# A relational graph layer on one core: inner Winograd products from the second matrix on, edge counts in half a PSUM bank, and relation counts from the slot table

## The chip, the cores and the metric

One core of one Trainium2 chip. The metric is the device time of one execution of the program in microseconds (us), as a median over runs. A profile is one execution of the same program with the hardware profiler on; its times are shown in microseconds from the span's start. In its rows PE is TensorE's matmuls, PEld its weight loads, DVE is VectorE, ACT is ScalarE, POOL is GpSimd, and SP is SyncE, which here only issues DMAs.

## The reference

There are N = 1250 nodes with D = 1024 features, and E = 20000 edges with a source, a destination (sorted) and one of R = 8 relations. Everything is fp32.

```python
h = relu(layernorm(x))
out = h @ root + bias
for r in range(8):                       # mean over the edges of relation r into each node
    mask = (edge_type == r)
    sums = segment_sum(h[src] * mask[:, None], dst, N)
    cnt  = segment_sum(mask, dst, N)
    out += (sums / max(cnt, 1)[:, None]) @ weight[r]
u = out
z = concat([u, h], axis=1) @ w_gate + b_gate
y = x + tanh(u) * z + h * (1 - z)
```

## The kernel before

**Products first, edges after.** The kernel multiplies all nodes by each matrix and gathers rows of the products afterwards: `h @ weight[r]` goes to DRAM (`y0` for relations 0 to 4, `y1` for 5 to 7), and each edge later fetches one row of it, scaled by one over its count. There are eleven matrices: eight relations (matrix zero to seven), `root`, and two halves of `w_gate`. Nodes are ten blocks of 128 rows (`ND`), taken as five pairs i = 0 to 4, block i with block i + 5.

**Winograd's scheme, twice.** `product` multiplies two blocks of rows (256 x 1024) by one matrix (1024 x 1024) with seven quarter products instead of eight: `p1` to `p7`, each of a left factor (A11, A12, A22, S1 to S4, in `h_op`) and a right factor (in `wbuf`), with K = 512 and 512 columns, so four fp32 matmuls of 128x512 each. `Factors` makes the right sums T1 to T4 on VectorE. For two neighbouring i, and from matrix one on, some of the seven quarter products are joined over both i and split once more into 2x2 with seven inner products of two 128x256 matmuls each: class `Second` does A12 B21 so, in all matrices from one on; classes `Third` (S4 B22) and `First` (A11 B11) only where `thirds(s)` holds, which is `s > EARLY`, with EARLY = 3. These classes take their sums from VectorE, and ScalarE copies inner results between PSUM and SBUF in the middle of the chain: `First.early` and `First.late` are two halves of one inner product, the early one at the end of the `product` before; `Third.first` writes into the PSUM bank `ps_q`, and `Third.hold` uses `ps_n`. The other PSUM banks are four of `ps` and two of `ps_b` (`lead`).

**Work beside the products.** The order is written out by hand. `product` calls `done()` after each quarter product (and after some fills, the pieces of inner products put between them), which calls `between(j)`; that takes one step of a generator. So there are seven steps in each `product`, and whatever a generator emits up to its `yield` lies behind that piece of TensorE's work on every engine's own queue. From matrix zero to three the generator is `index()`: `columns` and the layer norms, then `slots`, then `order`.

**The edge index (`slots`).** Edges stand in 157 chunks of 128; four chunks make a group (`CG`), so there are 40 groups, and a group takes two steps. The index gives each edge its place among the edges of its key (node and group of relations, 20 blocks of keys). In a group, `one_hots` makes bf16 one-hot matrices (ScalarE for `is_lo`, VectorE for `is_at`), `count` multiplies them (four matmuls of 128x100: 20 columns for keys and 80 for relation and block), `seen` holds running counts by VectorE additions, `as_int`, `split` and `as_bf16` cut the counts into two bf16 parts, and `place` looks up each edge's count with four matmuls of 128x40, adds the rank within the chunk, and scatters edges into `table` in DRAM by indirect DMA, 28 slots for each key (`SLOTS`), and behind them the eight relation counts' reciprocals. The functions work on different groups in the same round:

```python
for j in range(ng + 3):
    for f, of in ((as_bf16, j - 3), (one_hots, j), (load_keys, j - 1), (as_int, j - 2),
                  (None, None), (count, j - 1), (split, j - 2), (place, j - 3),
                  (to_los, j - 2), (None, None)):
```

`(None, None)` is a `yield`. Counts are written into `ps_n`, look-ups into `ps_q`, one buffer each.

**After the index.** `order` ranks the nodes by count (`places`); `rows_and_weights` scatters the ranking and gathers each node's slots from `table` into `idx`; `weights` turns a slot's relation and the reciprocal counts into a factor for each slot. In matrix four the generator `beside_group` does this for both groups of relations; `passes_needed` decides, once, how many extra passes over the table are needed for nodes with many edges, and one branch (`tc.If`, L1443) does them if any. From matrix five on the edge phase runs: 193 gathers of rows of `y` by GpSimd's indirect DMA (L1294), each added by VectorE with its weight (L1299).

Of the kernel before, what the change touches and what calls it, by code (L numbers as in the profile page):

```python
# [9 lines left out]
F32 = mybir.dt.float32  # L10
# [9 lines left out]
def tile_rgcn_highway(  # L20
# [52 lines left out]
    WIDE = SLOTS + R  # L73
# [3 lines left out]
    NTB = R * ND  # L77
    FAR = 1 << 20
    CG = 4
    GOT = 5  # L80
# [34 lines left out]
    table = dram.tile([G * KEYS * WIDE, 1], I32, name="table")  # L115
# [142 lines left out]
    class Third:  # L258
# [31 lines left out]
        def first(self, p):  # L290
            self.b = psum.tile([P, CG, P], F32, name="ps_q", bufs=1).rearrange(
                "p c k -> p (c k)")[:, :H]
# [242 lines left out]
    def thirds(s):  # L535

        return s > EARLY

    waiting, waiting_third, waiting_first = {}, {}, {}
# [10 lines left out]
    def step(s, i, between=lambda j: None, second=None):  # L550
# [61 lines left out]
        def sums(j):  # L612


            e = waiting[0][0]
            for k in {2: (0, 1), 4: (2, 3)}.get(j, ()) if s > EARLY else (j,) if j < 4 else ():
                e.right(k)
            if j == (5 if s > EARLY else 4):
                e.left()
# [82 lines left out]
    idx = const.tile([P, G, ND, WIDE], I32, name="idx")  # L702
    rcp = idx.bitcast(F32)[:, :, :, SLOTS:]
# [4 lines left out]
    n_pass = const.tile([1, 1], I32, name="n_pass")  # L708
    apart = const.tile([P, 1], F32, name="apart")
# [20 lines left out]
    def slot_weights(g, at, w, t, drc):  # L730

        n = at.shape[2]
        for r in range(R0[g], R0[g + 1]):
            by, to = rcp[:, g, :, r], w
            if r > R0[g]:
                by, to = drc, t
                nc.vector.tensor_sub(drc, rcp[:, g, :, r], rcp[:, g, :, r - 1])
# [3 lines left out]
            if r > R0[g]:  # L741
                nc.vector.tensor_add(w, w, t)
        nc.vector.scalar_tensor_tensor(w, at, float(FAR), w, op0=OP.is_lt, op1=OP.mult)

    table_rows = table.rearrange("(k s) o -> k (s o)", s=WIDE)
    more_rows = table_more.rearrange("(k s) o -> k (s o)", s=MORE)

    def rows_and_weights(g):
# [16 lines left out]
        for d in range(ND):  # L765
            rows_of(idx[:, g, d, :], table_rows, node_key[:, g, d:d + 1])
            if d % 2:
                yield

    with ExitStack() as early:  # L770
# [103 lines left out]
        far = ix0.tile([P, G * ND * WIDE // 4], I32, name="far")  # L874
# [44 lines left out]
        tb_col = ix1.tile([P, NCH], F32, name="tb_col")  # L919
# [7 lines left out]
        pid = ix1.tile([P, 1], F32, name="pid")  # L927
        less_pid = ix1.tile([P, 1], F32, name="less_pid")
        before = ix1.tile([P, P], F32, name="before")
        runs = ix1.tile([P, NHI + NTB], F32, name="runs")  # L930

        def columns():
# [23 lines left out]
            blk_i = ix0.tile([P, 2, P], I32, name="blk_i")  # L956
            nc.vector.tensor_single_scalar(blk_i, ed["dst"], 7, op=OP.arith_shift_right)
            blk = ix0.tile([P, 2, P], F32, name="blk")
            nc.vector.tensor_copy(blk, blk_i)
# [3 lines left out]
            for g in range(1, G):  # L963
# [5 lines left out]
            tb = ix0.tile([P, 2, P], F32, name="tb")  # L969
            nc.vector.scalar_tensor_tensor(tb, f["typ"], float(ND), blk,  # L970
                                           op0=OP.mult, op1=OP.add)
# [3 lines left out]
            for of, to in ((key, key_col), (row, row_col), (tb, tb_col)):  # L975
# [12 lines left out]
            nc.vector.tensor_single_scalar(first, key_col, float(WIDE), op=OP.mult)  # L988
# [8 lines left out]
        def slots(ix):  # L997
# [3 lines left out]
            seen = {-1: ix.tile([P, CG, NHI + NTB], F32, name="seen", bufs=3)}  # L1001
            nc.vector.memset(seen[-1][:, CG - 1, :], 0.0)
            ng = -(-NCH // CG)

# [3 lines left out]
            def one_hots(j):  # L1008
# [8 lines left out]
                is_at = ix.tile([P, CG, NHI + NTB], BF16, name="is_at", bufs=4)  # L1017
                for t, of, width in ((is_at[:, :, :NHI], hi_col, NHI),
                                     (is_at[:, :, NHI:], tb_col, NTB)):
                    nc.vector.tensor_tensor(t[:, :m, :],  # L1020
                                            of[:, c0:c1, None].to_broadcast([P, m, width]),
# [691 lines left out]
```

## Time and profile before

| | |
|---|---|
| Time, median of 3 runs | 1348.01 us (1346.19 to 1349.48) |
| The profiled execution's own time | 1347.63 us |
| Its span, first to last instruction | 1345.6 us |
| Matmuls of 128x512 into `ps_b` (L405) | x1560 rows, 701.9 us busy |
| Matmuls of 128x256 of inner products (L218) | 71.5 us busy in the largest of several groups |
| Counting matmuls (L1031) / look-ups (L1082) | x157 each, 13.6 / 10.1 us busy |
| VectorE additions to `seen` (L1036) | x157, 40.3 us busy, 257 ns each |
| ScalarE one-hots (L1013) | x157, 50.2 us busy |

How to read it: an fp32 matmul instruction shows as two rows, so x8 of 128x512 are the four of one quarter product. A row's own duration is the time through the array; matmuls overlap, so the price of one is the distance from its start to the next one's start. "Idle before" with a name behind an arrow says which instruction on which engine ended the wait. A timeline row merges equal instructions that follow each other: start, length, engine, line, operation, output<-inputs, shapes, count.

### The profile page before, as it was taken

What the parts mean: (1) busy time and instruction counts of PE and PEld (TensorE: products, weight loads), DVE (VectorE), ACT (ScalarE), POOL (GpSimd) and SP (SyncE); (2) the same over time, 40 slices, a digit from 0 to 9 for tenths busy, and PEclk for the clock granted to TensorE, in tenths of its full rate; (3) what the DMA queues carried; (4) which work ended last, traced back from release to release, by engine and by line L of the source; (5) the groups of instructions that cost most, each with busy time, mean ns of one, the idle gap of its engine ahead of it and who ended that gap; (6) DMA issues with size and microseconds to landing.
All of it is one profiled execution on the core that took longest, in us unless ns stands there. A gap on an engine that the chain in (4) does not pass through costs nothing.

```text
span 1345.6 us, 13662 instructions
## 1 busy us (share of the span) xinstructions
PE 1332.0 (99%) x4098; PEld 712.2 (53%) x4098; DVE 995.7 (74%) x2049; ACT 384.0 (29%) x852; POOL 579.9 (43%) x511
## 2 busy tenths in 40 slices
PE   9999999999999999999999999999999999999997
PEld 5444455455445545655654565565556556554443
DVE  7855976876784937524887978887788799867875
ACT  3335656565641111111221211112122111221210
POOL 0001755655563346101444646336354655625631
PEclk9999999999999999999999999999999999999999
DMA  8744665844673162133739778867878967879961
GB/s 313 271 181 145 105 135 148 209 81 124 160 183 83 49 171 53 48 126 122 234 114 349 223 254 326 310 230 268 286 260 291 343 211 234 288 275 283 345 171 59
DMA packets 106910, 271.17 MB, mean 202 GB/s; under 512 B 22692, under 2 KB 24946, under 8 KB 106704
## 3 DMA queue, kind: packets, MB, share of 16 engines
q1 hardware_dynamic: 46640, 120.01, 29.2%
q0 software_dynamic: 44064, 118.28, 27.9%
q10 hardware_dynamic: 16128, 31.98, 7.2%
q8 instruction: 32, 0.52, 0.2%
q14 instruction: 46, 0.38, 0.1%
HBM read 212.71 MB, written 75.66 MB: 214 GB/s over the span
## 4 chain that ended last, share of the span: by engine, by line
PE 79%; issue 7%; DMA 7%; DVE 4%; POOL 3%; ACT 0%; POOLq 0%; DVEq 0%; ACTq 0%
PE ps_b L405 40%; PE ps L405 17%; PE ps L218 11%; DMA got<-y,idx 5%; PE ps_n L405 3%; PE ps_b L218 2%; PE ps_q L218 2%; PE ps_q L405 1%; DVE u L1299 1%; PE ps_n L218 1%; POOL got L1294 1%; DMA got<-hr_dram,node 1%; PE ps L370 1%; DMA hr_dram<-row 1%; POOL out_dram L720 1%
## 5 line engine op out<-in xcount | busy, mean ns | idle before, releaser
L405 PE MATMUL ps_b<-w,h_op 128*128 128x512 f32 x1560 | 701.9, 595 | 1.0 <-ACT row L484 0.8
L405 PEld LDWEIGHTS ps_b<-w,h_op 128*128 128x128 f32 x1560 | 291.6, 190 | 329.2 <-issue 318.7
L1294 POOL DMA_INDIRECT got<-y,idx x193 | 246.3, 1276 | 326.4 <-DVE u L1299 195.8
L1299 DVE SCALAR_TENSOR_TENSOR u<-got,w_of,u 128x1024 f32<-128x1024 f32 (+1 forms) x193 | 247.1, 1283 | 33.8 <-DMA got<-y,idx 31.1
L405 PE MATMUL ps<-w,h_op 128*128 128x512 f32 (+1 forms) x592 | 263.4, 588 | 1.0 <-ACT row L464 1.0
L1110 POOL DMA_INDIRECT table<-row_col,at_i x157 | 177.7, 1132 | 156.4 <-DVE at_i L1106 70.3
L405 PEld LDWEIGHTS ps<-w,h_op 128*128 128x128 f32 x592 | 111.3, 190 | 125.0 <-issue 120.8
L430 DVE TENSOR_TENSOR row<-row 128x512 f32<-128x512 f32 x53 | 36.7, 693 | 72.9 <-ACT row L429 72.7
L429 ACT COPY row<-ps_b 128x512 f32<-128x512 f32 x53 | 31.0, 585 | 197.4 <-PE ps_b L405 193.4
L514 ACT COPY row<-ps_b 128x512 f32<-128x512 f32 x49 | 28.6, 584 | 200.3 <-PE ps_b L405 171.5
L405 PE MATMUL ps_n<-w,h_op 128*128 128x512 f32 x176 | 80.1, 592 | 0.0
L218 PE MATMUL ps<-w,w 128*128 128x256 f32 x288 | 71.5, 381 | 0.3 <-DVE w L211 0.3
L484 ACT COPY row<-ps_b 128x512 f32<-128x512 f32 x54 | 31.6, 586 | 135.9 <-PE ps_b L405 131.1
L218 PE MATMUL ps<-w,h_op 128*128 128x256 f32 x264 | 68.3, 381 | 0.0
L218 PEld LDWEIGHTS ps<-w,w 128*128 128x128 f32 x288 | 54.2, 190 | 21.9 <-issue 14.6
L1036 DVE TENSOR_TENSOR seen<-seen,ps_n 128x100 f32<-128x100 f32 x157 | 40.3, 257 | 30.1 <-PE ps_n L1031 10.1
L218 PEld LDWEIGHTS ps<-w,h_op 128*128 128x128 f32 x264 | 49.6, 190 | 24.3 <-issue 18.7
L1096 DVE SCALAR_TENSOR_TENSOR junk<-k_bc,key_col,before 128x128 f32<-128x128 int32 x157 | 55.1, 351 | 4.2
L453 ACT COPY row<-ps_b 128x512 f32<-128x512 f32 x54 | 31.7, 587 | 90.9 <-PE ps_b L405 82.9
L405 PEld LDWEIGHTS ps_n<-w,h_op 128*128 128x128 f32 x176 | 33.4, 190 | 39.5 <-issue 38.7
L464 ACT COPY row<-ps 128x512 f32<-128x512 f32 x37 | 21.6, 585 | 105.2 <-PE ps L405 92.6
L173 DVE TENSOR_TENSOR w<-w,w 128x2048 f32<-128x2048 f32 (+1 forms) x12 | 25.4, 2115 | 35.1 <-PE ps L405 34.9
(244 smaller groups left out, 1530.6 us busy)
## 6 DMA issues: line engine op xcount, KB each, us to landing
y<-row SPq DMA_DIRECT2D x72, 512.0 KB
w<-in_L_gnn_weight_dram ACTq DMA_DIRECT2D x21, 1024.0 KB
w<-in_L_gnn_weight_dram SPq DMA_DIRECT2D x10, 1024.0 KB
k_bc<-keys_dram SPq DMA_DIRECT2D x39, 256.0 KB
l_bc<-los_dram SPq DMA_DIRECT2D x39, 256.0 KB
w<-in_L_gnn_w_gate_dram ACTq DMA_DIRECT2D x6, 1024.0 KB
h_dram<-h_op SPq DMA_DIRECT2D x9, 512.0 KB
u<-in_L_gnn_bias_dram SPq DMA_DIRECT2D x9, 512.0 KB
```

The costliest lines, as they stand in the source:

```text
L218: nc.tensor.matmul(p, a[:, k, :], b[:, k, :], start=(fresh and k == 0), stop=(k == 1), skip_group_check=True)
L405: nc.tensor.matmul(b[:, at], aop[:, i, k, :], w.of[i][:, k, at], start=(fresh and k == 0), stop=(k == KQ - 1), skip_group_check=True)
L429: nc.scalar.copy(d, b)
L430: nc.vector.tensor_add(c22, c22, d)
L453: nc.scalar.copy(c11, b)
L484: nc.scalar.copy(c12, b)
L514: nc.scalar.copy(c21, b)
L1036: nc.vector.tensor_add(seen[j][:, i, :], was, p[:, i, :])
L1096: nc.vector.scalar_tensor_tensor(junk, o["k_bc"][:, i, :], key_col[:, c:c + 1], before, op0=OP.is_equal, op1=OP.mult, accum_out=rank[:, c: ...
L1110: ins = nc.gpsimd.indirect_dma_start(out=table[:, :], out_offset=bass.IndirectOffsetOnAxis(ap=at_i[:n, i:i + 1], axis=0), in_=row_col[:n, ...
L1294: nc.gpsimd.indirect_dma_start(out=t[:n], out_offset=None, in_=y[g][:, :], in_offset=bass.IndirectOffsetOnAxis(ap=at[:n, d, k:k + 1], axis=0),
L1299: nc.vector.scalar_tensor_tensor(u[:n], t[:n], w, u[:n], op0=OP.mult, op1=OP.add)
```

## The change

It does four things.

- **Inner products from matrix one on.** `thirds(s)` is `s > 0` for `s > EARLY`; so A11 B11 and S4 B22 of the first two pairs of i get inner products in matrices one to three too. Their SBUF room is taken from the start on, and the T sums and left sums of `Second` lie at other steps there.
- **Counts by key alone.** The 80 columns for relation and block go, with all that made them (`tb`), so a count is 128x20. `seen` is a ring of twelve chunks. The two parts of a count are made without integers: a bf16 copy (ScalarE) and the residue (VectorE).
- **Half a bank, on zeros.** Counts and look-ups both lie in the right half of the bank `ps_q`, in matmuls that add to what is there; `clear`, a ScalarE copy of a zero, wipes 240 columns in each round. The left half is that of `Third.first`. `ps_n` is free for `Third.hold`.
- **Relation counts from the slot table.** In matrix four `slot_counts` counts, for each key, how many slots are at or above each relation's first row; reciprocals and slot weights follow in the last pair of matrix four. Nodes with more edges than slots are counted by a second branch (`counts_over`) ahead of it. The scatter to the table goes in bursts of four groups (`AT`).

The diff, cut to its core:

```diff
-            self.b = psum.tile([P, CG, P], F32, name="ps_q", bufs=1).rearrange(
-                "p c k -> p (c k)")[:, :H]
+            self.b = (q_bank[0] if q_bank else psum.tile([P, CG, P], F32, name="ps_q", bufs=1)
+                      .rearrange("p c k -> p (c k)"))[:, :H]
...
     def thirds(s):
-        return s > EARLY
+        return s > 0
...
-            for k in {2: (0, 1), 4: (2, 3)}.get(j, ()) if s > EARLY else (j,) if j < 4 else ():
+            for k in {2: (0, 1), 4: (2, 3)}.get(j, ()):
                 e.right(k)
-            if j == (5 if s > EARLY else 4):
+            if j == 5:
                 e.left()
...
+    def slot_counts(g, at, t, cum, to):
+        n = R0[g + 1] - R0[g]
+        nc.vector.memset(cum[:, :, 0:1], float(at.shape[2]))
+        for r in range(1, n + 1):
+            nc.vector.tensor_single_scalar(t, at, float(r * N), op=OP.is_ge)
+            nc.vector.reduce_sum(cum[:, :, r:r + 1], t, axis=AX.X)
+            yield
+        nc.vector.tensor_sub(to[:, :, R0[g]:R0[g + 1]], cum[:, :, :n], cum[:, :, 1:n + 1])
...
+            RING = 3 * CG
+            seen = ix.tile([P, RING, NHI], F32, name="seen", bufs=1)
+            counted = q_bank[0][:, H:H + CG * NHI].rearrange("p (c b) -> p c b", b=NHI)
+            looked = q_bank[0][:, H + CG * NHI:H + 3 * CG * NHI].rearrange(
+                "p (c a b) -> p c a b", a=2, b=NHI)
+
+            def clear():
+                nc.scalar.copy(q_bank[0][:, H:H + 3 * CG * NHI],
+                               zero.to_broadcast([P, 3 * CG * NHI]))
...
             def count(j):
                 cs, o = chunks(j), now[j]
-                p = psum.tile([P, CG, P], F32, name="ps_n", bufs=1)[:, :, :NHI + NTB]
-                for i in range(m):
-                    nc.tensor.matmul(p[:, i, :], o["is_lo"][:, i, :], o["is_at"][:, i, :],
-                                     start=True, stop=True)
...
+                for i in range(len(cs)):
+                    nc.tensor.matmul(counted[:, i, :], o["is_lo"][:, i, :], o["is_at"][:, i, :],
+                                     start=False, stop=True, skip_group_check=True)
+                for i, c in enumerate(cs):
+                    nc.vector.tensor_add(seen[:, c % RING, :], seen[:, (c - 1) % RING, :],
+                                         counted[:, i, :])
...
             def place(j):
-                p = psum.tile([P, CG, P], F32, name="ps_q", bufs=1).rearrange("p c k -> p (c k)")
                 for i in range(m):
-                    nc.tensor.matmul(p[:, i * 2 * NHI:(i + 1) * 2 * NHI], o["to_lo"][:, i, :],
+                    nc.tensor.matmul(looked[:, i].rearrange("p a b -> p (a b)"),
+                                     o["to_lo"][:, i, :],
                                      o["s_b"][:, i].rearrange("p a b -> p (a b)"),
-                                     start=True, stop=True)
+                                     start=False, stop=True, skip_group_check=True)
...
             for j in range(ng + 3):
-                for f, of in ((as_bf16, j - 3), (one_hots, j), (load_keys, j - 1), (as_int, j - 2),
-                              (None, None), (count, j - 1), (split, j - 2), (place, j - 3),
+                for f, of in ((one_hots, j), (load_keys, j - 1), (as_bf16, j - 2),
+                              (None, None), (count, j - 1), (residue, j - 2), (place, j - 3),
                               (to_los, j - 2), (None, None)):
                     if f is None:
                         yield
                     elif 0 <= of < ng:
                         f(of)
+                    if f is as_bf16:
+                        clear()
...
         def beside_group():
+            for _ in range(4):
+                yield
+            passes_over()
+            yield
+            yield from rows_and_weights(1)
+            yield
+            yield
             for g in range(G):
-                if g:
-                    yield from rows_and_weights(g)
-                    yield
-                    yield
-                weights(g)
+                yield from counts(g)
+
+        def weights_of_groups():
+            as_reciprocals()
+            yield
+            for g in range(G):
+                yield from weights(g)
                 yield
             yield from passes_needed()
...
         while s < R0[1]:
             step(s, i, on)
             s, i = next(steps)
+            if (s, i) == (R0[1] - 1, NP - 1):
+                for _ in ready:
+                    pass
+                counts_over()
+                ready = weights_of_groups()
```

## The prediction

> **What bounds the kernel now.** I read the page first, then TensorE's waits, then the granted clock and busy time by stretch, then the timeline of the stage in which the changed code runs.
>
> ```profile
> PE 1332.0 (99%) x4098; PEld 712.2 (53%) x4098; DVE 995.7 (74%) x2049; ACT 384.0 (29%) x852; POOL 579.9 (43%) x511
> PE   9999999999999999999999999999999999999997
> PEclk9999999999999999999999999999999999999999
> ```
>
> TensorE has something in flight in 99% of the span, in every slice but the last, at full granted clock. So every microsecond of matmul taken out can be won, and every wait put in front of TensorE is lost whole. Its waits in the whole run:
>
> ```profile
> PE ps L697 <- POOL eps L699: 1.4, 1, 1.4
> PE ps_q L1082 <- ACT s_b L1066: 1.4, 1, 1.4
> ```
>
> The list is seven lines long and 5.8 us in all; only one wait belongs to the edge index, one look-up at L1082. The index runs from 107 to 420 us beside the products. Matrix one and matrix four, by stretch (length, then busy time of PE, PEld, DVE, ACT, POOL):
>
> ```profile
> 140.50:264.00 123.50, 123.50 (x431) 61.72 (x430) 96.98 (x412) 75.81 (x201) 74.47 (x70) 1.00 0.68 149
> 506.00:622.00 116.00, 116.00 (x354) 66.50 (x353) 57.47 (x127) 21.40 (x43) 24.88 (x23) 1.00 0.25 83
> ```
>
> Matrix four already has the inner products that the change gives to matrices one to three, and takes 7.5 us less; but there VectorE is at 50% and ScalarE at 18%. In matrix one, with the index beside it, they are at 79% and 61%. How the index lies between the products now (start, length):
>
> ```profile
> 146.99 0.34 PE L1031 MATMUL ps_n<-is_at,is_lo 128*128 128x100 bf16 x4
> 147.17 0.26 PE L1082 MATMUL ps_q<-s_b,to_lo 128*128 128x40 bf16 x4
> 147.27 3.68 PE L405 MATMUL ps_b<-w,h_op 128*128 128x512 f32 x8
> 148.14 1.13 DVE L1036 TENSOR_TENSOR seen<-seen,ps_n 128x100 f32<-128x100 f32 x4
> ...
> 150.79 1.03 PE L218 MATMUL ps<-w,h_op 128*128 128x256 f32 x4
> 150.99 0.58 ACT L484 COPY row<-ps_b 128x512 f32<-128x512 f32 x1 [1.94 <-PE ps_b L405]
> ...
> 151.65 0.34 PE L1031 MATMUL ps_n<-is_at,is_lo 128*128 128x100 bf16 x4
> 151.69 0.70 ACT L1013 ACTIVATE is_lo<-io,less_lo 128x128 bf16<-128x128 f32 x2
> ```
>
> Four counts, four look-ups 0.18 us later, and the next product 0.10 us after that: 0.28 us a group, although VectorE reads the counts only at 148.14. The look-ups need nothing of these counts (they are for the group two before) and write another bank. This freedom is what the change gives up.
>
> **The change, part by part.**
>
> *Inner products.* A11 B11 and S4 B22 of two pairs in each of matrices one, two and three: 12 products, each 14 matmuls of 256 columns for 8 of 512. Four 512-wide instructions (x8 in the rows) follow each other in 3.43 us, 0.858 each; two 256-wide (x4) in 0.86, 0.430 each. 8 x 0.858 - 14 x 0.430 = 0.85 us; twelve give **-10.2 us**.
>
> *Narrower counts.* 157 matmuls of 20 columns for 100. Four counts take 0.18 us, four look-ups of 40 columns 0.10; at the look-ups' price 157 x (0.045 - 0.025) = 3.1 us, and the two transposes of `tb` (0.4 us at 46.8) go: **-3.5 us**. TensorE's work falls by 13.7.
>
> *The shared bank.* Counts and look-ups go into the right half of the bank `ps_q`, and the inner S4 B22 product into its left half. In the instruction order of the changed program the first look-up of each group still stands directly behind the group's four counts, but it now waits for VectorE, namely for the last of the four `seen` additions that read those very counts; this is so in all 38 groups that have both. Behind it on TensorE is the next product, and everything else. The price from the row where VectorE had nothing else to do:
>
> ```profile
> 196.90 0.34 PE L1031 MATMUL ps_n<-is_at,is_lo 128*128 128x100 bf16 x4
> 197.08 0.26 PE L1082 MATMUL ps_q<-s_b,to_lo 128*128 128x40 bf16 x4
> 197.28 1.13 DVE L1036 TENSOR_TENSOR seen<-seen,ps_n 128x100 f32<-128x100 f32 x4 [1.94 <-PE ps_n L1031]
> ```
>
> The additions start 0.38 us after the first count. With 20 columns for 100 each is shorter by 80 x 1.04 ns (a 512-wide addition takes 0.685, a 256-wide 0.42), so four end after 0.80 us for 1.13: at 198.08, and the look-up starts 0.05 later (the gap seen where TensorE waited for an engine: the copy's end at 1077.73, weight load at 1077.79). 198.13 for 197.08 is 1.05 us; 38 groups give **+40 us**. None of it has cover: TensorE's queue is in order.
>
> The Trainium skill's page "PSUM — Partial Sum Buffer", section "PSUM bank collisions raise a hardware error", says to guard PSUM by bank (and quadrant of partitions) and not by address, since two engines in one bank collide even in different columns. No run here shows a collision. Were only addresses to count, the sum would be the 13.7 us gained; by the page's rule the waits above are needed.
>
> *VectorE behind.* The 1.05 us holds when VectorE is idle; the first row above shows 148.14 - 146.99 = 1.15 us to the start, and another group had 175.76 - 173.39 = 2.37. For each of 39 intervals between groups I added the VectorE instructions queued in the changed order (durations from the groups by form) and set them against TensorE's work in the interval. Example, the sixth group: residue 0.24, own and sum 0.64, four ranks 1.74, four index steps 0.66, two T sums 1.37, one-hot 0.23, two row additions 0.85, the four sums for the next inner product 2.21: 7.94 against TensorE's 4.49, 3.45 late. Twelve intervals are late, **22 us** in all. The index itself got cheaper on VectorE (a group from 5.1 to 3.75 us: narrower one-hots and additions, one residue for two splits, index steps per four groups), some 54 us over 39 groups; the sums and additions of the inner products put 12 us on each of the pairs, 71 in all, most of it in the index's stretch.
>
> *ScalarE behind.* Before, the step ahead of a group's look-ups began with the cast that they need (L1066); now it runs four one-hots 1.28, their Relu 0.63, the copy of `seen` 0.24 and the new zeroing of the half bank (128x240; 128x256 costs 0.36): 2.5 us, and the next counts wait for that zeroing. Where a whole product lies between, 3.43 us cover it. Where only a fill of 0.86 us lies between, as in the rows at 150.79, they don't: copy 0.59 + 2.5 + hand-over 0.27 - 0.86 = 2.5 us. Nine groups stand so: some 24 us. Four times the inner product's first matmul into `ps_q` meets the same zeroing (some 14), and six early and late inner parts wait for a ScalarE copy that stands behind the burst (some 6). Together **44 us**; VectorE catches up meanwhile. With the larger of the two in each interval the sum is 54; the bounds are 22 (ScalarE wholly hidden) and 66 (no overlap). I take 50, near the interval count, since a TensorE that waits gives both queues some air.
>
> *Nothing on the path:* counts from the slot table (8 comparisons and sums, some 1 us each on VectorE, in matrix four with 58 us free), weights moved to the end of matrix four (three VectorE instructions per step of TensorE; their first use is in matrix five), the fourfold scatter bursts on GpSimd (16 x 1.29 us in some 30; the last has 13 scatters, 17 us, and the gather that needs them comes after four steps and ten `places` of 1.55 us, some 29 us), the missing DMA of relation counts to the table. The second branch: the first now costs TensorE a load and 0.23 us at 972.9 while its matmuls go on at 0.86 us steps, so 0; if its cover is gone, 1 us.
>
> *Sum:* the profiled execution took 1347.6 us (span 1345.6 and 2.0 around it), 0.4 below the median of 1348.0. 1347.6 - 13.7 + 40 + 50 = **1424 us**.
>
> **Rivals.**
> 1. *Only the floor counts.* While TensorE waits, VectorE and ScalarE work off their queues, and the late intervals shrink to about 8: 1347.6 - 13.7 + 40 + 8 = 1382. For it: neither engine is over 80% in the stretch, and a longer period gives both more. Against: the bursts are emitted right ahead of the group and after the product that releases them, so a pause elsewhere doesn't move them.
> 2. *Faster: the wait is met before it is reached.* If the readout is over within 14 us / 38 = 0.36 us of the last count, the matmuls decide and the time is 1334. Against: four dependent additions with 0.25 us before the first; the shortest seen is 1.38 us with 100 columns.
> 3. *Both queues feed each other.* ScalarE's zeroing waits for VectorE's reading of the look-ups, VectorE's for TensorE, TensorE's inner products for sums that stand behind ranks. With no overlap (66) and 15 us of such second-order waits: 1455.
> That the change isn't what it says: its matmul counts (96 fewer of 512, 168 more of 256) say that it is.
>
> **How the numbers follow.** Forecast 0.70; rival 1 0.16; rival 3 0.09; rival 2 0.04; 0.01 that gain and waits cancel. What a measurement here can tell from no change is about 0.2%, 2.7 us. The range runs from rival 1 (1380) to rival 3's value (1455). Faster 0.04, same 0.01, slower 0.95.
>
> **What would show it.** TensorE's waits should name VectorE's `seen` some 38 times at 1.05 us and more, and ScalarE's zeroing of `ps_q` ten times or so at 2 to 3 us; TensorE's slices should read 7 or 8 from 110 to 480 us and 9 after; matrix one should take 150 us or more, matrix four as now. Wrong would be: look-ups that follow the counts in under 0.3 us (rival 2), waits of 1.0 to 1.3 us throughout (rival 1), or a loss after 500 us, in which case the moved weights or the second branch cost what I put at nothing.

## The result, and the profile after

| | median | range | ratio to before |
|---|---|---|---|
| before | 1347.9 us | 1346.2 to 1349.5 | |
| changed, as recorded | 1520.8 us | 1514.1 to 1523.5 | 1.1276, 95% interval 1.1237 to 1.1315 |
| changed, unaltered, on chip 6 ("the second chip" below) | 1471.3 us | 1468.6 to 1475.2 | 1.0944, 1.0925 to 1.0964 |
| changed, unaltered, on chip 4 | 1513.3 us | 1510.6 to 1524.0 | 1.126, 1.1224 to 1.1295 |

The change makes the kernel slower, as forecast, but by 173 us and not by 76; the recorded time lies far above the range. The two reruns say that some 50 us of the 173 are not the program's alone: chip 6 ran without them, chip 4 with them, which is taken up below. Which chip the recorded run had is not on record. Without these 50 us the time is still above the range.

The page of the recorded run (busy time and share of each engine; the span in 40 slices of 38 us):

```profile
PE 1372.7 (90%) x4240; PEld 760.0 (50%) x4240; DVE 1018.5 (67%) x2012; ACT 395.8 (26%) x859; POOL 572.1 (38%) x510
PE   9998677668775779899999999999999999999997
PEclk9999888789988799999999999999999999999999
```

TensorE's row drops to between 5 and 8 from the fourth slice to the fifteenth. The granted clock drops with it, which the prediction didn't have. By stretch (length, then busy time of PE, PEld, DVE, ACT, POOL; granted clock, DMA share, GB/s): the stretch that begins with the counts at 146.99 and ends with those at 264.61 before (117.6 us), and matrix four (116.0 us before):

```profile
156.78:359.51 202.73, 140.89 (x461) 78.72 (x460) 94.38 (x359) 75.43 (x189) 64.55 (x64) 0.83 0.37 86
679.00:795.00 116.00, 116.00 (x355) 66.51 (x354) 58.71 (x120) 21.44 (x43) 27.55 (x26) 1.00 0.24 83
```

The first takes 203 us for 118, and TensorE works 141 of them. Matrix four takes what it took. TensorE's waits (us in total, times, longest):

```profile
PE ps_q L1095 <- DVE seen L1050: 74.8, 36, 10.0
PE ps_q L1047 <- ACT ps_q L1022: 15.5, 8, 3.8
PE ps_b L217 <- ACT ps_b L343: 6.2, 2, 4.9
PE ps_q L217 <- ACT ps_q L1022: 6.1, 2, 3.1
```

L1095 is the look-ups, L1050 the additions of counts, L1047 the counts, L1022 the zeroing, L217 the inner products. The first line is the wait that the prediction put first, 36 times. One group, to be read against the groups shown before:

```profile
186.12 0.26 PE L1047 MATMUL ps_q<-is_at,is_lo 128*128 128x20 bf16 x4 [2.91 <-ACT ps_q L1022]
186.49 0.17 DVE L1050 TENSOR_TENSOR seen<-seen,ps_q 128x20 f32<-128x20 f32 x1 [6.18 <-PE ps_q L1047]
186.88 0.59 DVE L1050 TENSOR_TENSOR seen<-seen,ps_q 128x20 f32<-128x20 f32 x3 [0.21 <-DVE seen L1050]
...
187.52 0.29 PE L1095 MATMUL ps_q<-s_b,to_lo 128*128 128x40 bf16 x4 [1.14 <-DVE seen L1050]
```

The counts wait 2.9 us for ScalarE's zeroing, the look-ups 1.1 us for VectorE's four additions. Before, the same eight matmuls took 0.28 us.

**An account of TensorE's time.** For each matmul I took the distance to the next one's start, and what it has above the undisturbed distance of its shape (0.429 us for 512 columns, 0.2155 for 256). Where a product matmul takes up to twice its distance, the excess is counted as half speed, otherwise as a stall.

| us | stalls | half speed | profiled execution |
|---|---|---|---|
| before | 10.3 | 7.8 | 1347.6 |
| changed, second chip | 120.1 | 32.5 | 1468.6 |
| changed, recorded | 159.0 | 45.6 | 1520.6 |

The column of half speed also catches small excesses that have nothing to do with the clock: the kernel before has 7.8 us there at a granted clock of 1.00 (7 to 1341 us), and none of its product matmuls takes about twice its distance. So only what lies above 7.8 is the clock's.

With the 13.7 us of work taken out, the second chip should be 109.8 + 24.7 - 13.7 = 120.8 us above before, and is 121.0; the recorded run should be 38.9 + 13.1 = 52.0 above that, and is 52.0. On the second chip the largest waits are these:

```profile
PE ps_q L1095 <- DVE seen L1050: 56.3, 38, 4.2
PE ps_q L1047 <- ACT ps_q L1022: 17.6, 9, 2.9
PE ps_q L217 <- ACT ps_q L1022: 9.6, 4, 3.0
```

So three things are to be explained: the stalls, the half speed, and what differs between chips.

### The profile page after: what moved, and what is told of

It is laid out like the page before. It is cut to its first block, busy times and chain, and to the rows that moved or that the text cites. A ratio compares the mean times of both kernels' runs of the same rounds, so it can differ in the third digit from the quotient of the medians.

```text
span 1518.8 us, 13834 instructions
## 1 busy us (share of the span) xinstructions
PE 1372.7 (90%) x4240; PEld 760.0 (50%) x4240; DVE 1018.5 (67%) x2012; ACT 395.8 (26%) x859; POOL 572.1 (38%) x510
## 4 chain that ended last, share of the span: by engine, by line
PE 67%; DVE 10%; issue 9%; another core or an unknown queue 5%; DMA 4%; ACT 3%; POOL 2%; POOLq 0%; DVEq 0%; ACTq 0%; SPq 0%
PE ps_b L404 32%; PE ps L404 11%; PE ps L217 11%; PE ps_n L404 4%; PE ps_b L217 3%; PE ps_q L217 3%; DVE seen L1050 2%; DMA got<-y,idx 1%; PE ps_q L404 1%; PE ps_n L217 1%; DVE junk L1172 1%; ACT is_lo L1033 1%; POOL got L1308 1%; PE ps L369 1%
## 5 line engine op out<-in xcount | busy, mean ns | idle before, releaser
L404 PE MATMUL ps_b<-w,h_op 128*128 128x512 f32 x1464 | 680.5, 611 | 1.0 <-ACT row L483 0.8
L1126 POOL DMA_INDIRECT table<-row_col,at_i x157 | 163.4, 1041 | 352.9 <-DVE at_i L1122 289.3
L404 PE MATMUL ps<-w,h_op 128*128 128x512 f32 (+1 forms) x448 | 202.2, 595 | 1.7 <-ACT row L463 1.7
L404 PEld LDWEIGHTS ps<-w,h_op 128*128 128x128 f32 x448 | 85.8, 193 | 97.1 <-issue 92.1
L404 PE MATMUL ps_n<-w,h_op 128*128 128x512 f32 x224 | 102.3, 593 | 0.0
L428 ACT COPY row<-ps_b 128x512 f32<-128x512 f32 x53 | 31.1, 586 | 243.4 <-PE ps_b L404 220.1
L1050 DVE TENSOR_TENSOR seen<-seen,ps_q 128x20 f32<-128x20 f32 x157 | 27.3, 174 | 93.3 <-PE ps_q L1047 47.2
L513 ACT COPY row<-ps_b 128x512 f32<-128x512 f32 x49 | 28.7, 586 | 227.6 <-PE ps_b L404 170.2
L1095 PE MATMUL ps_q<-s_b,to_lo 128*128 128x40 bf16 x157 | 10.6, 186 | 81.6 <-DVE seen L1050 74.8
L217 PE MATMUL ps<-inner,inner 128*128 128x256 f32 x288 | 78.1, 396 | 2.0 <-DVE inner L278 2.0
L217 PE MATMUL ps<-w,h_op 128*128 128x256 f32 x288 | 79.3, 400 | 0.0
L217 PE MATMUL ps<-w,w 128*128 128x256 f32 x288 | 73.1, 387 | 0.2 <-DVE w L210 0.2
L483 ACT COPY row<-ps_b 128x512 f32<-128x512 f32 x54 | 31.7, 586 | 157.8 <-PE ps_b L404 150.8
L217 PEld LDWEIGHTS ps<-w,h_op 128*128 128x128 f32 x288 | 56.5, 199 | 25.4 <-issue 18.7
L217 PEld LDWEIGHTS ps<-inner,inner 128*128 128x128 f32 x288 | 57.5, 200 | 18.7 <-issue 7.7
L217 PEld LDWEIGHTS ps<-w,w 128*128 128x128 f32 x288 | 55.4, 194 | 22.1 <-issue 14.3
```

Of the source, the lines that this page charges most:

```text
L217: nc.tensor.matmul(p, a[:, k, :], b[:, k, :], start=(fresh and k == 0), stop=(k == 1), skip_group_check=True)
L404: nc.tensor.matmul(b[:, at], aop[:, i, k, :], w.of[i][:, k, at], start=(fresh and k == 0), stop=(k == KQ - 1), skip_group_check=True)
L428: nc.scalar.copy(d, b)
L483: nc.scalar.copy(c12, b)
L513: nc.scalar.copy(c21, b)
L1050: nc.vector.tensor_add(seen[:, c % RING, :], seen[:, (c - 1) % RING, :], counted[:, i, :])
```

## The experiments

Theory A: what costs is the order of the accesses to the shared bank. Theory B: it is VectorE and ScalarE, late through the inner products' sums and copies. The letters in the texts on record are these. The kernel before ran beside all of them, on three chips, at 1345.3 to 1347.3 us (medians); the chip is named by the number that the runs list.

### Which edit costs: the bank, its order, the inner products (chip 15)

Look-ups ahead of the counts (`ahead`):

```diff
-  (None, None), (count, j - 1), (residue, j - 2), (place, j - 3),
+  (None, None), (look, j - 3), (count, j - 1), (residue, j - 2), (place, j - 3),
   # look: the four look-up matmuls that stood at the head of place
```

> The look-ups' matmuls are put ahead of the group's counts; both stay in the shared half bank, the early inner products stay. Theory A (the order in the shared bank: the first look-up waits for VectorE's readout of the counts just made): 86 us of TensorE's stalls go, and with them most of the 46 us of half-speed matmuls, some 35: 1521 - 86 - 35 = 1400 us. Theory B (the two queues are late because of the inner products, and the bank only shows where): the lateness comes back at the next access to the bank, at the zeroing; at most the floor of 40 goes: 1480 us.

Measured 1402.7 us (1398.6 to 1403.6), ratio 1.0401 (1.0375 to 1.0427). TensorE's waits:

```profile
PE ps_q L1094 <- ACT ps_q L1022: 19.6, 12, 3.3
PE ps_q L217 <- ACT ps_q L1022: 11.6, 4, 4.0
PE ps_q L217 <- DVE own L1103: 4.7, 3, 2.3
```

The wait for `seen` is gone from the list, and what is left names the zeroing. That this is theory A's number is luck: it was counted from the recorded 1521 us, 50 of which chip 15 doesn't show (below). Against the 1471.3 us of the changed kernel on a chip like it, 69 us are gone and not 121. Counted from there, theory B's bound (at most the floor of 40 goes) would be 1431 us, and the time is 28 us below it.

No inner products in matrices one to three (`shared_no_inner`), the shared half bank as in the change:

```diff
 def thirds(s):
-    return s > 0
+    return s > EARLY       # and the sums' times as before
```

> The early inner products are taken out, the shared half bank, the zeroing and the order in it stay. Theory A: 38 look-ups still wait 1.05 us each or somewhat more, 40 to 55 us, some half speed after it: 1348 - 3.5 + 40 to 60 = 1385 to 1405 us, waits on VectorE's seen near 38. Theory B: without the inner products' sums and copies nothing is late: 1345 to 1352 us.

Measured 1427.7 us (1426.4 to 1428.6), ratio 1.0599 (1.0579 to 1.0619); stalls 78.8, half speed 21.6 us.

```profile
PE ps_q L1095 <- DVE seen L1050: 55.1, 38, 4.2
PE ps_q L1047 <- ACT ps_q L1022: 7.7, 5, 2.1
```

Above theory A's interval and far from theory B's: 38 waits, as said, but with a mean of 1.45 us in this list, though VectorE has none of the early inner sums.

Separate banks as well (`apart_no_inner`): counts in `ps_n`, look-ups in `ps_q`, no zeroing.

```diff
-  nc.tensor.matmul(counted[:, i, :], ..., start=False, stop=True, skip_group_check=True)
+  counted = psum.tile([P, CG, P], F32, name="ps_n", bufs=1)[:, :, :NHI]
+  nc.tensor.matmul(counted[:, i, :], ..., start=True, stop=True)    # looked likewise in ps_q
```

> Early inner products out, counts and look-ups each in a bank of its own as before; narrower index counts, relation counts from the slot table and scatters in bursts stay. Theories A and B: 1348 - 3.5 = 1344 us. Theory D (the moved weights, the table counts or the scatter bursts cost something): over 1350 us.

Measured 1342.0 us (1340.7 to 1347.4), ratio 0.997 (0.9953 to 0.9986). So the shared bank, in the order of the change, costs 1427.7 - 1342.0 = 85.7 us without any inner product, and the narrower counts bring 4.1 us for the 3.5 forecast; table counts and moved weights cost nothing that this could tell.

Shared bank, no inner products, look-ups ahead, and the zeroing ahead of the one-hots (`ahead_no_inner`, the diff above and the next one below on `shared_no_inner`):

> Early inner products out, the shared half bank and its zeroing stay, look-ups ahead of the counts and the zeroing ahead of the one-hots. Theory A (only the order in the shared bank costs): at most 5 us above the kernel with separate banks, 1342 to 1347 us. Theory E (sharing a bank costs by itself, by accesses that keep each other out): 1355 us or more.

Measured 1343.0 us (1341.6 to 1348.2), ratio 0.9988 (0.9976 to 0.9999); stalls 8.3, half speed 7.8 us, both as in the kernel with separate banks. Two kinds of matmuls and their readouts can share a bank for 1 us, which the scatter of these runs doesn't tell from nothing. All but that 1 of the 85.7 us was order: of the look-ups and of the zeroing, which were moved together here.

With the inner products, look-ups ahead and zeroing ahead (`ahead_clear_first`):

```diff
 for j in range(ng + 3):
+    clear()
     for f, of in ((one_hots, j), ...
-        if f is as_bf16:
-            clear()
```

> As the kernel with the look-ups ahead, and the zeroing stands ahead of the four one-hots on ScalarE rather than behind them. If ScalarE's lateness (28 us of stalls before counts and inner products that wait for the zeroing) is its place in the queue, some 20 us more go than with the look-ups ahead alone: 1380 us by theory A. If the zeroing itself waits for VectorE's reading of the look-ups (theory B), the same time as there, within 5 us.

Measured 1383.0 us (1381.7 to 1388.3), ratio 1.0261 (1.024 to 1.0282): 20 us below `ahead`, so ScalarE's place in the order counts. It is still 40 us above the kernel without inner products, though these take 10.2 us of work out. Stalls are 51.6 us; of TensorE's waits, those for accesses to `ps_q` (zeroing, `own`, the inner product's readout and copy) are 24.3 us.

The zeroing ahead alone (`clear_first`), look-ups behind the counts as in the change:

> The changed kernel with the zeroing of the half bank ahead of the four one-hots on ScalarE, all else as it is, the look-ups still behind the counts. By theory A the 86 us at the look-ups stay; of some 28 us that counts and inner products wait for the zeroing some 20 go, with a few us of half speed: 1521 - 25 = 1495 us. If the zeroing's place were the larger part (theory C: ScalarE is what makes everything late, VectorE's waits included), under 1460 us.

Measured 1453.5 us (1451.1 to 1457.1). My expectation was counted from the recorded 1521 us, and by that this would have spoken for theory C. It doesn't: chip 15 shows none of the late completions (below), and against the changed kernel on a chip like it, 1471.3 us, it is 18 us, near the 25 expected. The look-ups wait 6.9 us more than there (68.8 for 61.9), so a part was handed on.

### VectorE's backlog

The four rank instructions of each group done twice (`double_ranks`): 51 us more of VectorE's busy time (1018.4 to 1069.8).

```diff
     accum_out=rank[:, c:c + 1])
+ for i, c in enumerate(cs):
+     nc.vector.scalar_tensor_tensor(again, o["k_bc"][:, i, :], key_col[:, c:c + 1], before,
+                                    op0=OP.is_equal, op1=OP.mult, accum_out=rank2[:, i:i + 1])
```

> The changed kernel with the four rank instructions of each group done twice (1.74 us more on VectorE a group, the second result is not used). If VectorE's backlog sets the waits above 1.05 us (22 of the 38 are above 1.5 us by the trace), 20 to 30 groups pass on 1.0 to 1.74 us each, and some 10 us of half speed come with it: 1550 to 1580 us. If the waits above the floor come from signals that arrive late or from ScalarE, under 1535 us.

Measured 1481.7 us (1480.6 to 1483.8, chip 15): 10 us above the 1471.3 of the changed kernel on chip 6, where 30 to 60 above the recorded time were expected. The look-ups' waits grow by 4 us in all, 61.9 to 66.0. VectorE's sum of work in an interval is not what makes it late. What is, one of the long waits shows (changed kernel, second chip):

```profile
305.33 0.25 PE L1047 MATMUL ps_q<-is_at,is_lo 128*128 128x20 bf16 x4
...
305.53 2.29 DVE L172 TENSOR_TENSOR w<-w,w 128x2048 f32<-128x2048 f32 x1 [4.67 <-PE ps L404]
307.74 0.80 DVE L1050 TENSOR_TENSOR seen<-seen,ps_q 128x20 f32<-128x20 f32 x4
308.45 0.30 DVE L1080 TENSOR_TENSOR s_b<-seen,s_b 128x20 bf16<-128x20 f32 x2
308.58 0.25 PE L1095 MATMUL ps_q<-s_b,to_lo 128*128 128x40 bf16 x4 [3.01 <-DVE seen L1050]
```

VectorE stood idle for 4.67 us. Then the product that stands just ahead of the counts releases a 2.29 us instruction that stands ahead of the additions. What VectorE had to do earlier had all that idle time to be done in; what TensorE releases in the same moment as the counts is what the look-ups wait for.

### Half speed

Five small matmuls that nobody reads, between counts and look-ups, in the kernel without early inner products (`shared_fill5`). The first try had ten (`shared_fill`).

```diff
+  idle = psum.tile([P, CG, P], F32, name="ps_n", bufs=1)
+  for _ in range(5):
+      nc.tensor.matmul(idle[:, 0, :], ident, ident, start=True, stop=True)
```

> The kernel without early inner products and with the shared half bank; between a group's counts and its look-ups ten small matmuls (some 1.09 us by their spacing of 0.109) are put that nobody reads, into a bank that is free there, so that TensorE works while VectorE reads. They fit into the 1.1 us that every look-up waits there. If idle stretches trip the clock gate (14 us of half speed there): 1428 - 14 = 1414 us, no half-speed spell but behind longer waits. If the gate has another reason: 1428 us, with the spells still there. If the wait isn't one that covers work: 1428 + 41 = 1469 us.

Measured 1455.9 us (1452.8 to 1457.0): my price was wrong, one such matmul takes two records of 0.112 us, so ten took 2.24 us and were a delay of their own. Half speed did fall, from 21.6 to 9.9 us.

> As the kernel with ten small matmuls between counts and look-ups, but with five: the trace has one at 0.223 us (two records of 0.112 each), so ten took 2.24 us, twice the wait they were to fill; five take 1.12 us and just fill it. If half speed comes of the idle stretches: 1428 us of the kernel without them less its 14 us of half speed, 1414 us. If the gate has another reason, 1428 us.

Measured 1420.7 us (1419.4 to 1424.5, chip 6), 7.0 below the kernel without them (chip 15). Half speed falls from 21.6 to 10.3 us, with 7.8 in the kernel before; stalls and filling (40 times 1.12 us) together are some 6 us above the stalls of the kernel without filling (the profiled execution is 5.5 us shorter, and half speed alone makes 11.3). The same wait costs less when TensorE is busy in it, and ten small matmuls took half speed away too, though they lengthened the whole. What sets the clock down, the trace shows (changed kernel, second chip, three windows from one change of the granted clock to the next, columns as above):

```profile
306.08:309.49 3.41, 0.91 (x6) 0.56 (x6) 3.15 (x10) 1.28 (x3) 2.81 (x2) 1.00 0.97 267
309.49:312.90 3.41, 3.41 (x5) 1.33 (x4) 3.30 (x14) 0.00 (x0) 2.70 (x3) 0.50 1.00 94
312.90:316.31 3.41, 3.41 (x9) 1.52 (x8) 0.14 (x1) 2.18 (x6) 0.98 (x1) 1.00 0.46 62
```

This is the wait of 3 us shown above: TensorE works 0.91 us in the first window, and in the next, though always busy, it gets half the clock and starts five rows, then nine at full clock.

### What differs between chips

The recorded trace has waits like this one (timeline of the recorded run):

```profile
324.14 0.25 PE L1047 MATMUL ps_q<-is_at,is_lo 128*128 128x20 bf16 x4
...
330.17 0.98 POOL L1126 DMA_INDIRECT table<-row_col,at_i  x1 [0.30 <-issue]
330.70 0.59 ACT L463 COPY row<-ps 128x512 f32<-128x512 f32 x1 [6.87 <-remote]
330.70 2.29 DVE L172 TENSOR_TENSOR w<-w,w 128x2048 f32<-128x2048 f32 x1 [11.03 <-remote]
...
333.58 0.80 DVE L1050 TENSOR_TENSOR seen<-seen,ps_q 128x20 f32<-128x20 f32 x4 [0.59 <-remote]
...
334.44 0.29 PE L1095 MATMUL ps_q<-s_b,to_lo 128*128 128x40 bf16 x4 [10.05 <-DVE seen L1050]
```

It is the same place as the row at 305.33 above. The product's last matmul ended at 324.3, but ScalarE and VectorE, which both wait for it, start together at 330.70, 6.3 us late, and "remote" says that the profile found no instruction that ended when the wait did. The trace's record of semaphores has the update that both wait for, one of TensorE's, at 330.67, and the next, for the counts that ended at 324.39, at 333.49. Meanwhile GpSimd issues scatters, sixteen in a row (310.8 to 331.1).

Rerun of the changed kernel (`again`, chip 6; `again2`, chip 4), the changed kernel with one more matmul at its start (`shifted`, chip 6), and with the scatters per group (`at1`, chip 6):

```diff
- for _ in range(IDLE):           # shifted
+ for _ in range(IDLE + 1):
- AT = 4                          # at1
+ AT = 1
```

> The changed kernel unaltered. In its trace eight completions of TensorE reach VectorE or ScalarE 2 to 7 us late (33 us of stalls beyond those of the kernel with doubled ranks), which none of the eight experiments so far shows. If that belongs to this program: 1514 to 1524 us again, with late completions at 282, 334, 390, 423, 472 and 522 us. If it belonged to the one chip or the hour it ran on: some 1480 us.

> The changed kernel with one more small matmul among the twelve at its start, which nobody reads: TensorE's instruction stream is shifted by one matmul, all else is as it is. If the late completions hang on the place of instructions in the program (or are the chip's of that hour): 1475 to 1490 us. If they come from what the kernel does at those times, the scatter bursts with which they coincide: 1515 to 1525 us.

> The changed kernel with the scatters issued per group, four at a time, rather than sixteen per four groups (and VectorE's index steps per group: 0.5 us more a group). If the bursts hold TensorE's completions back: 33 us of stalls and some half speed go, 1475 to 1490 us. If they don't: 1515 to 1530 us.

> The changed kernel unaltered once more. The recorded result (1521 us) and its rerun (1471 us) differ by 50 us, and only the recorded trace has late completions of TensorE. If these belong to one chip: 1471 us here, no late completions, unless this is that chip. If they come and go with the hour on any chip: anything from 1470 to 1520, with late completions where it is above 1480.

Measured: `again` 1471.3 us (1468.6 to 1475.2), `shifted` 1475.2 (1469.2 to 1477.4), `at1` 1468.0 (1466.2 to 1472.7), ratios 1.0944, 1.0958 and 1.0918 with overlapping intervals, and in none of the three traces a late completion; `again2` on chip 4 1513.3, with them. So the shift says nothing, the bursts cost nothing on chip 6, and the recorded run is like chip 4's. The last five kernels ran on chip 4. Inner products of A11 B11 alone, with separate banks (`first_only`, six products), and the kernel `ahead_clear_first` with inner products from matrix three on (`late_inner`, four products):

```diff
  # first_only, on apart_no_inner; product takes First without Third
- if thirds(s) and i == 1: return s, 2
+ if s > 0 and i == 1: return s, 2
- if coming and i > 1 and j == 2:
+ if coming and (i > 1 or not q) and j == 2:
  # late_inner, on ahead_clear_first
-     return s > 0
+     return s > 2
```

> Counts and look-ups in separate banks (the kernel of 1342 us), and of the early inner products only A11 B11, six products in matrices one to three, which use neither of these banks. Theory A (the shared bank makes the inner products dear; VectorE and ScalarE alone can carry them): 1342 - 6 x 0.85 + 0 to 3 = 1337 to 1340 us. Theory B (inner products beside the index cost by the load they put on VectorE and ScalarE): 1350 us or more.

> The shared half bank with look-ups ahead of the counts and the zeroing ahead of the one-hots, and the inner products from matrix three on, where only the last eight steps of the index are left. By theory A 1343 - 4 x 0.85 + 0 to 5 = 1340 to 1345 us; if inner products cost by themselves, 1350 us or more.

Measured 1403.7 us (1403.0 to 1407.5) and 1400.3 us (1392.9 to 1401.4): missed by 60 us, with waits up to 11 us for completions that came late. The same two with `AT = 1`, and the kernel with separate banks once more:

> Separate banks, of the early inner products only A11 B11, and the scatters issued four at a time per group. On a chip with late completions: if they come of the bursts of sixteen, 1345 to 1370 us, few of them left, for 1404 with bursts; if not, 1400 us again. On a chip without them: theory A (inner products are dear only by the shared bank) 1337 to 1340 us, theory B (by the load on VectorE and ScalarE) 1350 us or more.

> Shared half bank, look-ups and zeroing ahead, inner products from matrix three on, scatters four at a time per group. On a chip with late completions: if they come of the bursts, 1345 to 1370 us for 1400 with bursts; if not, 1400 us. On a chip without: theory A 1340 to 1345 us, theory B 1350 us or more.

> The kernel with separate banks and without early inner products once more, with the scatters in bursts of sixteen. On a chip without late completions 1342 us again. On a chip with them: if they cost only where TensorE waits for VectorE anyway, 1342 to 1350 us; if the bursts alone make TensorE wait, 1370 us or more, and then this kernel isn't better than the one before on every chip.

Measured on chip 4: 1356.3 us (1349.8 to 1362.2), 1353.1 us (1344.4 to 1358.6), and `apart_again` 1381.2 us (1377.2 to 1383.1), ratio 1.0244 (1.0221 to 1.0266). The last is the very program that took 1342.0 us on chip 15. What stands against VectorE and ScalarE in its lists of waits has no counterpart there, and one wait of TensorE's is 8.5 us long, where the same entry is 0.8 us there:

```profile
DVE seen L1041 <- remote: 35.0, 4, 11.5
ACT row L513 <- remote: 39.7, 5, 12.7
PE ps_b L404 <- ACT row L483: 9.3, 2, 8.5
```

and its timeline on chip 4:

```profile
237.16 1.11 PE L217 MATMUL ps<-w,h_op 128*128 128x256 f32 x4
...
240.57 0.98 POOL L1120 DMA_INDIRECT table<-row_col,at_i  x1 [0.30 <-issue]
243.62 0.58 ACT L463 COPY row<-ps 128x512 f32<-128x512 f32 x1 [11.75 <-remote]
243.77 0.80 DVE L1041 TENSOR_TENSOR seen<-seen,ps_n 128x20 f32<-128x20 f32 x4 [5.16 <-remote]
```

The counts of 236.96 are read at 243.77, when a burst (220.9 to 241.5) has ended; here TensorE has to wait for the readers of its banks. What is late is the report and not the work: four updates of TensorE's semaphore stand in the trace at 243.60, 243.69, 243.75 and 243.81, while the matmuls that were still unreported had ended at 233.69, 237.12, 237.21 and 237.32, and TensorE had started each following matmul at its usual distance. On chip 15 the three that end there at 237.34, 237.43 and 237.54 are reported within 0.02 us of their ends.

All 91 waits that end with "remote" in the five traces with bursts of sixteen on chip 4 and in the recorded one end during a scatter or at most 2.5 us behind one. The twelve traces of chips 6 and 15 have no such wait. Scatters issued four at a time take 47.5 us off `first_only` and 47.2 off `late_inner`. So on this chip the bursts of sixteen cost 39 us (`apart_again` against chip 15) to 47 us, whatever the rest of the kernel; with scatters four at a time, as in the kernel before, the chip is hardly slower than others (1347.3 and 1346.7 us before, for 1345.3 on chip 6). Why TensorE's completions are reported late beside such a burst, and only in some runs, stays open. Nor do the runs separate chip from hour: chips 15, 6 and 4 were each used in one stretch of time, one after the other, though the kernel before took its usual time beside the slow ones.

Also open: whether the early inner products bring their 0.85 us each where they share no bank. `first_only_at1` and `late_inner_at1` still contain late completions, in places where the groups' scatters run together into rows of 8 to 20 (the first has 19.9 us of stalls for 10.3 before), their best runs are 1349.8 and 1344.4 us, and neither ran on another chip.

No kernel here beats the one before everywhere: separate banks without early inner products do so on chip 15 by 0.3%, and lose 2.4% on chip 4.

## Why the prediction was wrong

The likeliest case named the right mechanism, the place and the sign. Its sum was 97 us short, in three terms: it put the scatter bursts and the clock at nothing, and took the lateness of VectorE and ScalarE 20 us too small (us; measured by the account of stalls and half speed, and by the runs):

| step | forecast | measured |
|---|---|---|
| inner products, narrower counts | -13.7 | -13.7 closes the account; the counts' part -4.1 in `apart_no_inner` for -3.5 |
| floor at the look-ups | +40 | 38 waits, none under 1.03 us: +40 |
| VectorE and ScalarE late | +50 (22 to 66) | on the second chip 22 more at the look-ups, 24 at the counts, 24 at inner products and readouts: +70 |
| clock | 0 | +25 |
| scatter bursts | 0 | +52 in the recorded run, 0 on chips 6 and 15 |
| from matrix four on | 0 | 0 |

- **The bursts are the largest miss.** The prediction put "the fourfold scatter bursts on GpSimd" under "Nothing on the path", by the time that their results have until the gather. That was the wrong question: they cost by what runs beside them. In the recorded run and on chip 4 TensorE's completions come up to 10 us late while a burst runs, and much of that ends up in front of TensorE. The trace of before held a hint: one `seen` addition, at 175.76, with 4.59 us of idle time ended by "remote". The prediction read this very row (2.37 us from the counts to the addition) as VectorE being behind, but VectorE had nothing to do there.
- **The clock was left out.** "At full granted clock" was read as a property of the kernel; it was a property of a TensorE that never stood. The Trainium skill's page "TensorE: Matmul & The Clock Gate", section "Part 1: The HAM clock gate (the "warmup" mystery)", has a free-running window of 3413 ns in which activity is watched, and half the clock after an idle window. The spells in these traces are multiples of 3.41 us, as it says; but a window with 2 us of idle time was enough, not only an idle one. By the page's table a wait of 3 us costs nothing but itself; by the rows above it cost a window at half clock, some 1.7 us more. The measurement decides.
- **Lateness by queue sums was the wrong way to count.** The sum of 22 for VectorE agrees with 22 us above the floor at the look-ups, but by chance: 51 us of further work added 4 us there, and taking out the inner sums left those waits at 60.7 us (61.9 with them). What counts is what stands between the release and the addition in the one moment, as in the row of 2.29 us. The zeroing was rightly named (24 us of stalls at the counts, and 20 us come off when it moves ahead); nothing in the sum was meant for inner products waiting for `own` and for readouts of `ps_q`. And the overlap failed: 50 was taken because VectorE was to catch up while TensorE waits for ScalarE, but the waits stand one after another, in front of different matmuls, and make more than the 66 without any overlap.
- **The rivals.** Rival 1 (the floor only) fell with 120 us of stalls; rival 2 with the first group shown; rival 3's mechanism, inner products waiting behind VectorE's reading of the look-ups, is in the traces, but its 1455 us is below every run of the changed kernel. That a chance of 0.05 for faster or equal was small was right.
- **What would show it.** Right: `seen` named some 38 times, the zeroing about ten times at some 2 us, matrix one slower and matrix four as it was; the slices read 5 to 8. The loss reaches to 600 us rather than 480, because the index itself is stretched (its last counts are at 568.72, before at 402.45). It is not the moved weights or the second branch: from the start of matrix four to the end of the span it takes 839.8 us, before 839.6.

## What to carry to other kernels

When two tasks are put into one buffer, write down the order in which they touch it: two touches by TensorE with another engine's readout between them cost the readout each time, and putting the older task's touch first took 70 us off here (`clear_first` to `ahead_clear_first`) with nothing else changed. Price a wait in front of a TensorE that is 99% busy with what follows it, too: waits of 2 us and more brought half speed along, 25 us for 110 us of stalls. And before a sum is trusted, look for idle time ended by "remote": one such wait of 4.59 us stood in the trace before, and with the scatters bunched some 50 us of the recorded time came with such waits.

## What the runs showed of the hardware

- **The clock.** Cut into windows of 3.413 us as the clock's changes lie, the changed kernel's trace (second chip) has 18 windows with over 2.0 us of idle TensorE, and behind every one of them the granted clock is 0.5; it fell behind one window with less (1.84 us), and the largest idle time without consequence was 1.93 us. With the doubled ranks that was 2.00 us. Over all traces here the lowest idle time that set it down was 1.71 us (`ahead_clear_first`). One wait of 1.1 us in a window is free in this respect. Once down, less is enough to stay there: on the second chip the clock came back behind windows with at most 0.62 us of idle time and stayed at 0.5 behind one with 1.21, so a trip can cost more than one window.
- **A bank shared in the right order is free.** Two sets of matmuls and their readouts, by VectorE and ScalarE, in one half bank: 1343.0 us for 1342.0 with separate banks.
- **Chips, or hours, differ beside GpSimd's scatters.** One program took 1342.0 us on chip 15 and 1381.2 us on chip 4, while the kernel before differed by 0.6 us (1346.1 and 1346.7). What is held back are updates of TensorE's semaphore: 9.9 us in the longest case read above (from 233.69 to 243.60).
